# Reading one operand of VectorE's multiplications from PSUM, in a two-layer graph network on one core

## The chip, the cores and the metric

The kernel runs on one core of one Trainium2 chip. The metric is the device time of one execution in microseconds. TensorE multiplies matrices and writes PSUM, VectorE (DVE in the profile) and ScalarE (ACT) work element by element on SBUF and PSUM, GpSimd (POOL) issues the gathers, and SyncE (SP) issues the other transfers.

## What is computed

The reference is two layers of a relational graph convolution over 50,000 nodes with 128 features each, then a residual sum and a layer norm. There are 850,000 edges (50,000 of them self-loops), with 16 relations, whose matrices are combinations of 8 bases. Cut to what matters:

```python
def _rgcn_layer(h, src, dst, rel, basis, w_comp, loop_w, bias):
    W = jnp.einsum('rb,bio->rio', w_comp, basis)
    seg = dst.astype(jnp.int32) * N_REL + rel.astype(jnp.int32)
    agg = jax.ops.segment_sum(h[src], seg, num_segments=N_ENT * N_REL)
    agg = agg.reshape(N_ENT, N_REL, -1)
    msg = jnp.einsum('nri,rio->no', agg, W)
    out = msg + h @ loop_w + bias
    return jax.nn.relu(out)

h = _rgcn_layer(x, src, dst, edge_type, basis1, w_comp1, loop_w1, bias1)
h = _rgcn_layer(h, src, dst, edge_type, basis2, w_comp2, loop_w2, bias2)
out = _layernorm(x + h)
```

Edges are sorted by destination.

## The kernel before

Edges other than self-loops are cut into tiles of 128, and tiles into chunks of `K` = 10. A layer has 625 chunks, 6,250 tiles. For each tile POOL gathers the 128 source rows (line 250) into one of `GATHERS` = 4 buffers `g`, each a chunk long; the gathers of chunk c + 2 stand in the program at chunk c, and a gather waits until TensorE has read the same tile four chunks earlier.

A tile's destinations are at most `WN` = 12 neighbouring nodes. For each chunk, `hot_of` (lines 906 to 922) makes two things on VectorE. At line 909, `own`: for each edge, a 0/1 row that says which of the 12 nodes is its destination, by comparing `grid` (the numbers 0 to 11, a part of `col` in SBUF) with the edge's `key`. At line 916, `hot`: the product of `own` with the edge's 8 weights `pm`, one per basis, that is 960 numbers a partition. The program makes `hot` for chunk c two chunks early. TensorE multiplies a tile's gathered rows by its `hot` (line 1004) into a PSUM bank `pa`: 8 bases by 12 nodes, 96 columns; five tiles share a bank. VectorE then adds each tile's 96 columns into `ring` in SBUF at the place of its nodes (`add`, line 936).

`ring` holds three groups of 512 nodes. A group's share begins with its self-loops: `Group.own` (line 766) multiplies `wide` (the group's self-loop weights, spread over all partitions by a transfer of 1 MB from `CW`, four bases at a time) by `hT`, the transposed features of the group, broadcast over the four bases: 2,048 numbers a partition, twice a group, 98 groups a layer. When all chunks that touch a group are added, ScalarE copies its ring (line 783), TensorE multiplies by the bases (line 789) and by the loop matrix (line 794), ScalarE applies bias and relu (line 801), TensorE transposes back (line 813), and the rows are stored.

In the first layer, beside the chunks, VectorE also sorts edges and self-loops apart (`closed_up`, lines 317 to 330): it takes a bit of each word (line 326) into `bit` and copies by that predicate (line 329), 450 times each.

PSUM has eight banks of 512 columns. One is `pn`, for the bases. Seven turn as `pa`, handed out by `banks.take` (class `Turns`): it takes the oldest bank, and first emits the reading operations that were registered for that bank and have not been emitted yet, such as the adds of its five tiles. `Once` makes each of these run a single time, whether at its planned time or forced by `take`. Beside the tiles of a chunk, the weights of a batch of four chunks (`multiply`, two banks, copied out at line 678), the transposed features, the combined self-loop weights and the way back each take a bank.

The order of TensorE, POOL, VectorE and ScalarE is the order in which the program emits. Steps beside the chunks are put in a heap with the tile number at which they are due (`later`), and `go_on` emits those that are due after each tile; adds are emitted by `added_up_to`, some 25 tiles behind their matmul. Transfers on SP are ordered by a scheduler.

Of the kernel before, what the change touches and what calls it, by code (L numbers as in the profile page):

```python
# [40 lines left out]
F32 = mybir.dt.float32  # L41
I32 = mybir.dt.int32
BF16 = mybir.dt.bfloat16
# [5 lines left out]
PSUM = bass.MemoryType.PSUM  # L49
DRAM = bass.MemoryType.DRAM  # L50

P = 128
EPR = 850000
ROW = 10
WN = 12
K = P // WN
# [11 lines left out]
BANK = 512  # L68
WEIGHTS = AT * PER * 8
BITS_AT_ONCE = 224  # L70
# [6 lines left out]
BEHIND = 12  # L77
AFTER = 18
AT_ONCE = 4
# [10 lines left out]
def tile_rgcn_resnorm(  # L90
# [15 lines left out]
    nc = tc.nc  # L106
    N, D = x.shape
    NR, NB = w_comp1.shape
# [34 lines left out]
    consts = ctx.enter_context(tc.tile_pool(name="consts", bufs=1))  # L143
    col = consts.tile([P, P], F32, name="col")
# [3 lines left out]
    ident = consts.tile([P, P], F32, name="ident")  # L148
    nc.vector.tensor_scalar(ident, col, part, None, op0=OP.is_equal)

    grid = col[:, :WN]
    eps = consts.tile([P, 1], F32, name="eps")
    nc.vector.memset(eps, EPS)

# [64 lines left out]
                    left = less  # L219
            nc.vector.tensor_copy(split[:, n], mine)  # L220

    ps_a = ctx.enter_context(tc.tile_pool(name="ps_a", bufs=7, space=PSUM))
    ps_n = ctx.enter_context(tc.tile_pool(name="ps_n", bufs=1, space=PSUM))

    class Turns:
        def __init__(self, pool, name, count):
# [17 lines left out]
            if what is not None:  # L244
                what(*self.args)

    banks = Turns(ps_a, "pa", 7)

    def gather(to, of, idx):
        return nc.gpsimd.indirect_dma_start(  # L250
# [27 lines left out]
    picked = consts.tile([P, 5 * NG + 3 * len(ROWS)], F32, name="picked")  # L278
    ones = consts.tile([P, 1], F32, name="ones")
    place = consts.tile([P, RUN], F32, name="place")  # L280
    bit = consts.tile([P, BITS_AT_ONCE], I32, name="bit")

    odd_i = consts.tile([P, 1], I32, name="odd_i")
    nc.gpsimd.iota(odd_i, pattern=[[0, 1]], base=0, channel_multiplier=1)
# [318 lines left out]
    def chunked():  # L603
        with (
# [8 lines left out]
            def nodes(g):  # L613
                return min(GN, N - g * GN) // J
# [10 lines left out]
            class Weights:  # L625
                def __init__(self, c, n):
                    self.c, self.n = c, n
                    self.m = min(AT, 2 * (C - c)) * NR
                    self.keep = Once(self.kept)
# [58 lines left out]
            class Group:  # L688
                def __init__(self, g, of, n, copied):
                    self.g, self.of, self.n, self.copied = g, of, n, copied  # L690
                    self.m, self.cnt = nodes(g), nodes(g) * J
                    self.at = g % TURN * GN
                    self.wide, self.made = {}, False
                    self.keep, self.kept = Once(self.turned), Once(self.store, 0)
                    self.combined = Once(self.stored_comb)

# [55 lines left out]
                def widen(self, b):  # L752
# [7 lines left out]
                        ),  # L760
                    )

                def own(self, b):
                    cnt = self.cnt
                    assert self.g < TURN or self.copied[0] > self.g - TURN
                    nc.vector.tensor_tensor(  # L766
                        ring[:, b : b + AT_ONCE, self.at : self.at + cnt],
                        self.wide.pop(b)[:, :, :cnt],
                        self.hT[:, None, :cnt].to_broadcast([P, AT_ONCE, cnt]),
                        op=OP.mult,  # L770
                    )
                    self.made = b == NB - AT_ONCE
# [57 lines left out]
                        done(self.norm)  # L830
                        nc.sync.dma_start(of_group(out, g), self.t)

                def planned(self, later, free):
                    from_chunk = -(-(self.g * GN - NEAR) // (N // C)) - 1
                    start = K * from_chunk - 4
                    end = max(K * final(self.g) + K - 1 + BEHIND, free - AFTER + 1)
                    went = start - 2
                    if self.n == 0:
                        later(went - 78, self.load)
                        later(went - 66, self.turn)  # L840
                        later(went - 66 + BEHIND, self.keep)
                        later(went - 62, self.compare)
                        later(went - 48, self.combine)
                        later(went - 48 + BEHIND, self.combined)
                    else:
                        later(went - 40, self.load)
                    for i, b in enumerate(range(0, NB, AT_ONCE)):
                        later(went - 30 + 14 * i, self.widen, b)
                        later(went - 16 + 14 * i, self.own, b)
                    later(end, self.copy)  # L850
                    for b in range(NB):
                        later(end + AFTER + 2 * b, self.base, b)
                    end += AFTER + 2 * NB
                    later(end, self.loop)
                    later(end + BEHIND, self.relu)
                    later(end + BEHIND + AFTER, self.back)
                    later(end + 2 * BEHIND + AFTER, self.kept)
                    for step in range(1, 3 if self.n else 1):
                        later(end + 2 * BEHIND + AFTER + 3 * step, self.store, step)
                    return end + BEHIND  # L860
# [43 lines left out]
            for n, of in enumerate((x, H1)):  # L904

                def hot_of(c):
                    pm = batches[c // BATCH].pm
                    own = hp.tile([P, K, WN], BF16, name="own")
                    nc.vector.tensor_tensor(  # L909
                        own[:, : ks(c)],  # L910
                        grid[:, None, :].to_broadcast([P, ks(c), WN]),
                        key[:, c * K : c * K + ks(c), None].to_broadcast([P, ks(c), WN]),
                        op=OP.is_equal,
                    )
                    hot = hp.tile([P, K, NB, WN], F32, name="hot", bufs=4)
                    nc.vector.tensor_tensor(  # L916
                        hot[:, : ks(c)],
                        pm[:, c % BATCH * K : c % BATCH * K + ks(c), :, None].to_broadcast([P, ks(c), NB, WN]),
                        own[:, : ks(c), None, :].to_broadcast([P, ks(c), NB, WN]),
                        op=OP.mult,  # L920
                    )
                    hots[c] = hot
# [26 lines left out]
                def later(time, what, *args):  # L949
                    heapq.heappush(events, (time, len(order), what, args))  # L950
                    order.append(None)
# [17 lines left out]
                for batch in batches[1:]:  # L969
                    when = K * (batch.c - 3) + PER + 3  # L970
# [6 lines left out]
                free = 0  # L977
                for one in groups:
                    free = one.planned(later, free)
# [3 lines left out]
                for c in range(C):  # L983
# [16 lines left out]
                    for k in range(K):  # L1000
                        if k % PER == 0:
                            pa = banks.take(Once(added_up_to, c * K + k + PER - 1))
                        if k < ks(c):
                            nc.tensor.matmul(  # L1004
                                pa[:, k % PER * NB * WN : (k % PER + 1) * NB * WN],
                                g[:, k, :],
                                hot[:, k].rearrange("e b w -> e (b w)"),
                                start=True,
                                stop=True,
                            )  # L1010
                            behind.append((c * K + k + BEHIND, (c, k, pa)))
                        added_up_to(c * K + k - BEHIND)
                        if c or k >= BEHIND - 2:
                            go_on(c * K + k)
                    if n == 0 and c == 3:
                        beginning.close()
# [212 lines left out]
```

## Time and profile before

| | us |
|---|---|
| three timed executions | 18,116.25 to 18,146.69, median 18,145.05 |
| the profiled execution | 18,143.9 |
| its span, first to last instruction | 18,141.6 |

The profile is of one execution. A group's row names the line, engine, operation, tiles (out<-in) and count, then the busy time in us and the mean ns of one, then the time that the engine stood idle before them and what ended most of it. "issue" means that the profile shows nothing waited for, "remote" that the releaser is not known. A row of the timeline has the start, the length, what ran, how many in a row, and the idle time before the first. fp32 matmuls of lines 1004, 789, 794 and 664 show as two instructions each.

### The profile page before, as it was taken

What the parts mean: (1) busy time and instruction counts of PE and PEld (TensorE: products, weight loads), DVE (VectorE), ACT (ScalarE), POOL (GpSimd) and SP (SyncE); (2) the same over time, 40 slices, a digit from 0 to 9 for tenths busy, and PEclk for the clock granted to TensorE, in tenths of its full rate; (3) what the DMA queues carried; (4) which work ended last, traced back from release to release, by engine and by line L of the source; (5) the groups of instructions that cost most, each with busy time, mean ns of one, the idle gap of its engine ahead of it and who ended that gap; (6) DMA issues with size and microseconds to landing.
All of it is one profiled execution on the core that took longest, in us unless ns stands there. A gap on an engine that the chain in (4) does not pass through costs nothing.

```text
span 18141.6 us, 132343 instructions
## 1 busy us (share of the span) xinstructions
PE 8301.5 (46%) x31484; PEld 6157.8 (34%) x31484; DVE 6520.1 (36%) x18252; ACT 1406.4 (8%) x1864; POOL 12963.3 (71%) x12540
## 2 busy tenths in 40 slices
PE   3444444444444444444444444444444444445444
PEld 2333333333333333333333333333333333333333
DVE  4444444443333333333333333333333333333333
ACT  0000000000000000000000000000000000000000
POOL 6777777777777777777767777777777777777776
PEclk7666666666666666665655655655565556655565
DMA  3333333322222222222222222222222222222222
GB/s 100 95 93 92 93 94 94 94 90 88 80 85 84 85 84 85 85 85 81 84 79 80 81 81 79 81 84 76 81 84 78 81 81 81 81 81 81 81 81 67
DMA packets 793016, 1527.31 MB, mean 84 GB/s; under 512 B 229924, under 2 KB 296342, under 8 KB 792230
## 3 DMA queue, kind: packets, MB, share of 16 engines
q0 software_dynamic: 403552, 826.82, 15.8%
q1 hardware_dynamic: 386934, 691.33, 11.5%
q8 instruction: 260, 4.26, 0.1%
q14 instruction: 526, 4.31, 0.1%
q10 hardware_dynamic: 1744, 0.60, 0.0%
HBM read 1390.97 MB, written 126.86 MB: 84 GB/s over the span
## 4 chain that ended last, share of the span: by engine, by line
issue 37%; PE 22%; another core or an unknown queue 15%; POOL 14%; DMA 7%; DVE 3%; ACT 1%; DVEq 0%; POOLq 0%; ACTq 0%; SPq 0%
PE pa L1004 14%; POOL g L250 14%; PE pn L789 5%; DMA g<-H,src 4%; DMA g<-in_x_dram,src 3%; DVE ring L936 1%; PE pa L664 1%; ACT own L783 1%; PE pa L813 1%; PE pn L794 1%; DVE ring L766 1%; DVE word L329 0%; DVE bit L326 0%; DVEq L930 0%
## 5 line engine op out<-in xcount | busy, mean ns | idle before, releaser
L1004 PE MATMUL pa<-hot,g 128*128 128x96 f32 x25000 | 5869.2, 361 | 8329.8 <-issue 5856.8
L1004 PEld LDWEIGHTS pa<-hot,g 128*128 128x128 f32 x25000 | 5129.8, 269 | 10232.5 <-issue 7601.0
L250 POOL DMA_INDIRECT g<-in_x_dram,src x6250 | 6497.8, 1040 | 2549.3 <-issue 1150.2
L250 POOL DMA_INDIRECT g<-H,src x6250 | 6426.4, 1028 | 2549.6 <-issue 1167.7
L936 DVE TENSOR_TENSOR ring<-pa,ring 128x96 f32 x12500 | 3205.0, 256 | 10919.4 <-remote 5042.0
L789 PE MATMUL pn<-own,basis 128*128 128x512 f32 x3104 | 2062.1, 749 | 242.5 <-issue 193.9
L916 DVE TENSOR_TENSOR hot<-pm,own 128x960 f32<-128x960 f32 x1250 | 1457.5, 1166 | 90.8 <-remote 17.5
L783 ACT COPY own<-ring 128x4096 f32<-128x4096 f32 x194 | 699.4, 3605 | 5461.9 <-DVE ring L936 4142.0
L766 DVE TENSOR_TENSOR ring<-wide,hT 128x2048 f32<-128x2048 f32 x392 | 896.1, 2286 | 232.3 <-DMA wide<-CW 111.9
L789 PEld LDWEIGHTS pn<-own,basis 128*128 128x128 f32 x3104 | 601.6, 236 | 334.6 <-issue 287.0
L664 PE MATMUL pa<-each,is_rel 128*128 128x128 f32 x1570 | 375.3, 376 | 579.6 <-issue 380.6
L801 ACT ACTIVATE oT<-pn,bias_of 128x512 f32<-128x512 f32 x196 | 134.2, 685 | 6281.8 <-remote 2909.1
L664 PEld LDWEIGHTS pa<-each,is_rel 128*128 128x128 f32 x1570 | 312.7, 273 | 631.9 <-issue 467.7
L909 DVE TENSOR_TENSOR own<-col,key 128x120 bf16<-128x120 f32 x1250 | 341.9, 273 | 0.0
L813 PE MATMUL pa<-ident,oT 128*128 128x128 f32 (+1 forms) x784 | 215.5, 378 | 236.2 <-issue 190.1
L794 PE MATMUL pn<-hT,loop 128*128 128x512 f32 x392 | 251.8, 717 | 69.1 <-issue 69.1
L813 PEld LDWEIGHTS pa<-ident,oT 128*128 128x128 f32 (+1 forms) x784 | 147.8, 221 | 279.2 <-issue 271.5
L678 ACT COPY pm<-pa 128x192 f32<-128x192 f32 x628 | 142.7, 304 | 804.6 <-remote 635.0
L329 DVE COPY_PREDICATED word<-bit,word 128x224 int32<-128x224 int32 (+9 forms) x450 | 180.2, 400 | 37.6 <-DVE bit L326 11.5
L601 ACT ACTIVATE t<-t,nm,rs 128x128 f32<-128x128 f32 x392 | 161.3, 482 | 78.3 <-issue 36.1
L721 PE MATMUL pa<-ident,rows 128*128 128x128 f32 x392 | 102.2, 380 | 107.9 <-issue 71.2
L749 ACT COPY lrel<-pa 16x512 f32<-16x512 f32 x98 | 56.2, 574 | 1166.5 <-remote 599.9
(127 smaller groups left out, 1328.4 us busy)
## 6 DMA issues: line engine op xcount, KB each, us to landing
wide<-CW SPq DMA_DIRECT2D x388, 1024.0 KB
g<-in_x_dram,src POOLq DMA_INDIRECT x6250
g<-H,src POOLq DMA_INDIRECT x6250
rows<-in_x_dram SPq DMA_DIRECT2D x194, 256.0 KB
PM<-pm SPq DMA_DIRECT2D x157, 160.0 KB
pm<-PM SPq DMA_DIRECT2D x157, 160.0 KB
H1T<-oT SPq DMA_DIRECT2D x97, 256.0 KB
H<-t SPq DMA_DIRECT2D x97, 256.0 KB
```

The costliest lines, as they stand in the source:

```text
L250: return nc.gpsimd.indirect_dma_start(out=to, out_offset=None, in_=of, in_offset=bass.IndirectOffsetOnAxis(ap=idx, axis=0))
L329: moved = nc.vector.copy_predicated(word[:, a : a + k], bit[:, :k], word[:, a + step : a + step + k])
L664: nc.tensor.matmul(of[:, :, :, (j - j0) * NB : (j - j0 + 1) * NB], self.is_rel[:m, j * P : (j + 1) * P], each[:m], start=True, stop=True,)
L766: nc.vector.tensor_tensor(ring[:, b : b + AT_ONCE, self.at : self.at + cnt], self.wide.pop(b)[:, :, :cnt], self.hT[:, None, :cnt].to_broad ...
L783: nc.scalar.copy(self.sums, ring[:, :, at : at + cnt])
L789: nc.tensor.matmul(self.pn[:, : self.cnt], BASIS[:, b, :], self.sums[:, b, :], start=b == 0, stop=False)
L794: nc.tensor.matmul(self.pn[:, : self.cnt], LOOP, self.hT[:, : self.cnt], start=False, stop=True)
L813: nc.tensor.transpose(self.po[:m, j * D : (j + 1) * D], by_place[:, j, :], ident)
L909: nc.vector.tensor_tensor(own[:, : ks(c)], grid[:, None, :].to_broadcast([P, ks(c), WN]), key[:, c * K : c * K + ks(c), None].to_broadcast ...
L916: nc.vector.tensor_tensor(hot[:, : ks(c)], pm[:, c % BATCH * K : c % BATCH * K + ks(c), :, None].to_broadcast([P, ks(c), NB, WN]), own[:, ...
L936: nc.vector.tensor_tensor(into, pa[:, k % PER * NB * WN : (k % PER + 1) * NB * WN].rearrange("d (b w) -> d b w", w=WN), into, op=OP.add,)
L1004: nc.tensor.matmul(pa[:, k % PER * NB * WN : (k % PER + 1) * NB * WN], g[:, k, :], hot[:, k].rearrange("e b w -> e (b w)"), start=True, st ...
```

## The change

`grid` moves from SBUF into a PSUM bank of its own, `fixed`, which also holds `own` (two places that alternate by chunk, now 32-bit instead of bfloat16) and `bit`. So line 909 reads `grid` from that bank and writes `own` to it, line 916 reads `pm` from SBUF and `own` from PSUM, and line 329 reads its predicate from PSUM. For line 766 a new step `lay` on ScalarE copies the group's `hT` into a bank taken from the turning ones, once for each of the two multiplications of a group, 8 tiles ahead of it; the multiplication then reads `wide` from SBUF and the copy from PSUM, and is registered as that bank's reader. The turning banks become six. Steps of groups other than the first are due no earlier than tile 12, and in a layer's first chunk due steps are emitted after its last tile, where before none was.

```diff
-    grid = col[:, :WN]
...
-    ps_a = ctx.enter_context(tc.tile_pool(name="ps_a", bufs=7, space=PSUM))
+    ps_a = ctx.enter_context(tc.tile_pool(name="ps_a", bufs=6, space=PSUM))
+    ps_f = ctx.enter_context(tc.tile_pool(name="ps_f", bufs=1, space=PSUM))
+    fixed = ps_f.tile([P, BANK], F32, name="fixed")
     ps_n = ctx.enter_context(tc.tile_pool(name="ps_n", bufs=1, space=PSUM))
+
+    grid = fixed[:, :WN]
+    nc.vector.tensor_copy(grid, col[:, :WN])
...
-    banks = Turns(ps_a, "pa", 7)
+    banks = Turns(ps_a, "pa", 6)
...
-    bit = consts.tile([P, BITS_AT_ONCE], I32, name="bit")
+    bit = fixed[:, WN + 2 * K * WN : WN + 2 * K * WN + BITS_AT_ONCE].bitcast(I32)
...
-                    self.wide, self.made = {}, False
+                    self.wide, self.laid, self.made = {}, {}, False
+                    self.owns = {b: Once(self.own, b) for b in range(0, NB, AT_ONCE)}
...
+                def lay(self, b):
+                    self.laid[b] = banks.take(self.owns[b])
+                    nc.scalar.copy(self.laid[b][:, : self.cnt], self.hT[:, : self.cnt])
+
                 def own(self, b):
...
-                        self.hT[:, None, :cnt].to_broadcast([P, AT_ONCE, cnt]),
+                        self.laid.pop(b)[:, None, :cnt].to_broadcast([P, AT_ONCE, cnt]),
...
-                def planned(self, later, free):
+                def planned(self, queue, free):
+                    def later(when, *what):
+                        queue(max(when, BEHIND) if self.g else when, *what)
+
...
-                        later(went - 16 + 14 * i, self.own, b)
+                        later(went - 24 + 14 * i, self.lay, b)
+                        later(went - 16 + 14 * i, self.owns[b])
...
-                    own = hp.tile([P, K, WN], BF16, name="own")
+                    at = WN + c % 2 * K * WN
+                    own = fixed[:, at : at + K * WN].rearrange("e (k w) -> e k w", w=WN)
...
-                        if c or k >= BEHIND - 2:
+                        if c or k == K - 1:
                             go_on(c * K + k)
```

## The prediction

> **What bounds the kernel now.** I read the page's busy times first, then its groups, then the gathers' own rows, then waits and a timeline. The sum is made against the profiled execution: 18,143.9 us, of which the span is 18,141.6; the median of the three timed runs, 18,145.05, is the same within 0.01%.
>
> ```profile
> PE 8301.5 (46%) x31484; PEld 6157.8 (34%) x31484; DVE 6520.1 (36%) x18252; ACT 1406.4 (8%) x1864; POOL 12963.3 (71%) x12540
> ...
> L250 POOL DMA_INDIRECT g<-in_x_dram,src x6250 | 6497.8, 1040 | 2549.3 <-issue 1150.2
> L250 POOL DMA_INDIRECT g<-H,src x6250 | 6426.4, 1028 | 2549.6 <-issue 1167.7
> L936 DVE TENSOR_TENSOR ring<-pa,ring 128x96 f32 x12500 | 3205.0, 256 | 10919.4 <-remote 5042.0
> ...
> L916 DVE TENSOR_TENSOR hot<-pm,own 128x960 f32<-128x960 f32 x1250 | 1457.5, 1166 | 90.8 <-remote 17.5
> ...
> L766 DVE TENSOR_TENSOR ring<-wide,hT 128x2048 f32<-128x2048 f32 x392 | 896.1, 2286 | 232.3 <-DMA wide<-CW 111.9
> ...
> L909 DVE TENSOR_TENSOR own<-col,key 128x120 bf16<-128x120 f32 x1250 | 341.9, 273 | 0.0
> ```
>
> POOL is the busiest engine, and nearly all it does is 12,500 gathers. Their own rows, and a timeline stretch in the second layer:
>
> ```profile
> L250 POOL DMA_INDIRECT g<-in_x_dram,src x6250: 939/947/3060, 46.0 to 9117.1; - x196
> L250 POOL DMA_INDIRECT g<-H,src x6250: 939/947/3058, 9152.5 to 18093.2; - x196
> ```
> ```profile
> 12007.69 1.13 DVE L936 TENSOR_TENSOR ring<-pa,ring 128x96 f32 x4 [11.10 <-PE pa L1004]
> 12008.34 0.94 POOL L250 DMA_INDIRECT g<-H,src  x1 [0.30 <-DMA g<-H,src]
> ...
> 12008.74 0.27 DVE L909 TENSOR_TENSOR own<-col,key 128x120 bf16<-128x120 f32 x1
> 12009.04 1.16 DVE L916 TENSOR_TENSOR hot<-pm,own 128x960 f32<-128x960 f32 x1
> 12009.59 1.43 POOL L250 DMA_INDIRECT g<-H,src  x1 [0.30 <-issue]
> ...
> 12011.33 0.95 POOL L250 DMA_INDIRECT g<-H,src  x1 [0.30 <-issue]
> ```
>
> A gather takes 947 ns at the median (939 at least, 3,060 at most), and one follows another after 0.30 us: 1.25 us start to start. So 12,500 x 1.25 = 15,625 us would be enough. The rest is two things. The gathers' busy time is 6497.8 + 6426.4 = 12,924, which is 12,924 - 12,500 x 0.947 = 1,087 us more than the median gather would need. Their idle time is 5,099, which is 5,099 - 12,500 x 0.303 = 1,311 us more than the pipeline's own gap. 15,625 + 1,087 + 1,311 = 18,023; the first gather starts at 46 and the last one starts 48 us before the end, which leaves some 25 us for POOL's few other instructions.
>
> Where the 1,087 comes from is seen in the stretch: the gather at 12009.59 began while L916 ran, and ended 0.48 us late. The gather at 12008.34 began while L936 ran, and took 0.94. L916 reads two tiles in SBUF, L936 reads one of its two in PSUM. The long multiplication does the same, harder:
>
> ```profile
> 10413.85 0.94 POOL L250 DMA_INDIRECT g<-H,src  x1 [0.30 <-issue]
> ...
> 10418.55 2.29 DVE L766 TENSOR_TENSOR ring<-wide,hT 128x2048 f32<-128x2048 f32 x1
> 10418.85 2.81 POOL L250 DMA_INDIRECT g<-H,src  x1 [0.30 <-remote]
> 10420.87 0.37 SPq L754 DMA_DIRECT2D wide<-CW  x1
> 10420.88 0.84 DVE L936 TENSOR_TENSOR ring<-pa,ring 128x96 f32 x3
> ```
>
> L766 ends at 10420.84; the gather that met it ends at 10421.66, 0.82 us after it, late by 2.81 - 0.947 = 1.86.
>
> The 1,311 us of waits are of another kind: TensorE falls behind and POOL runs out of free buffers (four of ten tiles, so at most 40 tiles ahead).
>
> ```profile
> 10403.00:10455.00 52.00, 32.57 (x139) 24.04 (x139) 27.88 (x80) 6.24 (x7) 39.87 (x37) 0.73 0.32 99
> 10455.00:10495.00 40.00, 4.78 (x15) 4.02 (x14) 3.84 (x12) 0.69 (x1) 26.59 (x28) 0.50 0.23 65
> ```
> ```profile
> 10487.40 0.32 PE L1004 MATMUL pa<-hot,g 128*128 128x96 f32 x1 [2.48 <-issue]
> ...
> 10495.35 0.94 POOL L250 DMA_INDIRECT g<-H,src  x1 [5.39 <-remote]
> ```
>
> The columns of the windows are PE, PEld, DVE, ACT, POOL, each busy us (instructions), then the granted clock. In the 40 us from 10455 the clock was 0.50, TensorE did 15 matmuls (a tile needs two) and POOL 28 gathers, until a gather waited 5.39 us. Such stretches decide how much of a faster POOL is kept.
>
> **What the change does, part by part.**
>
> *L916, L909, L766 read one operand from PSUM.* Nothing is removed from VectorE. What goes, if the operand's place is what counts, is the lateness they give the gathers. Its size by geometry: a gather starts every 1.25 us, so an operation of d us catches one with probability d/1.25 and holds it d/2 on average, as long as d < 1.25; a longer one always catches one and holds it d - 0.62. L916: 1.166 x 1.166 / 2.5 = 0.54 us, x 1,250 = 680. L766: 2.286 - 0.62 = 1.66, x 392 = 652. L909: 0.273 x 0.273 / 2.5 = 0.03, x 1,250 = 37. That is 1,369, a quarter over the 1,087 that are there, so these three explain all of it; other two-input operations are short or few. I take 1,040 (96%).
>
> *Their own duration.* Two rows of 96 elements tell it, that of L936 above and this one:
>
> ```profile
> L777 DVE TENSOR_TENSOR ring<-ring 128x96 f32<-128x96 f32 x64 | 16.7, 260 | 2.2
> ```
>
> L936 takes 256 ns with one operand in PSUM, L777 260 with both in SBUF: no change. L909 now also writes the bank that it reads, which no row shows; even twice its 273 ns would be 342 us on an engine that idles 64% of the span, cover enough unless TensorE waits for the `hot` it makes. [...]
>
> *`lay`: 392 copies SBUF to PSUM on ScalarE.* The nearest row has the same 512 columns, out of PSUM:
>
> ```profile
> L821 ACT COPY t<-pa 128x512 f32<-128x512 f32 x97 | 57.0, 587 | 810.5 <-remote 601.3 <-PE pa L1004 199.2 <-PE pa L721 7.9
> ```
>
> 392 x 0.587 = 230 us on an engine that is 8% busy. It stands 8 tiles (10 us) ahead of the multiplication; behind it on ScalarE wait L801, L678 and the like, 0.6 us later. Free on the path.
>
> *Six banks instead of seven, and 392 more takes.* `take` forces the adds of the oldest bank out earlier, so TensorE runs with less room ahead of VectorE. The nearest row for a bank that is not free in time:
>
> ```profile
> DVE ring L936 <- remote: 5042.0, 367, 48.9
> ...
> DVE ring L936 <- PE pa L1004: 3639.2, 816, 30.2
> ...
> PE pa L1004 <- ACT pm L678: 523.6, 42, 51.1
> ```
>
> The columns are us in total, times, the longest. 314 banks that L678 empties (two for each of 157 batches) cost 523.6, 1.67 us a take; 392 more takes at that price are 654 us of TensorE, half of which POOL would feel. The other bound is 0, since VectorE empties the new banks within its own order, as it does those of L936. I take 30 us on POOL's path.
>
> *The start.* `bit` in PSUM takes the second SBUF input from 450 short L329s; events before tile 12 move by a few tiles once a layer. Within 20 us either way; 0 taken. POOL's order of gathers is untouched, and so is each queue's list of transfers.
>
> *How much of 1,040 is kept.* Where TensorE is the later one, an earlier POOL only waits longer at the 40-tile limit. All and nothing are the bounds. As a measure I take the time that L936 stood waiting for TensorE by the two rows above, 5042.0 (releaser not shown) + 3639.2 = 8,681 us, 48% of the span: 52% kept, 541 us. The stretches of slow TensorE seem to come in time, so 3% less time has 3% less of the 1,311: 39 us. Sum: 18,144 - 541 - 39 + 30 = 17,594, say 17,590.
>
> **Rivals.**
>
> *All kept, 17,100.* TensorE catches up between slow stretches every time (32.57 us busy out of 52 in the first window, at 139 matmuls for 37 gathers). 18,144 - 1,040 = 17,104, and down to 17,030 with fewer slow stretches. Against it: the lateness falls mostly while TensorE catches up, as after 10403.
>
> *TensorE paces everything, about 18,100.* POOL reaches the limit sooner and waits; 0 to 15% kept. Against it: POOL idles only 1,311 over its own gaps.
>
> *The operand's place is not what counts, 18,144.* A long VectorE operation may hold the gather whatever it reads; the trace has few long ones with a PSUM operand. Against it: the gather at 10413.85 and that at 12008.34 started inside runs of L936 and lost nothing. [...]
>
> *Banks run short, 18,350: slower.* Place: TensorE's wait for a bank at L1004, just while it catches up. If each of the 392 takes costs w us and half lands on POOL, the gain of 541 is gone at w = 2.8; at w = 4 it is 784 lost, 18,387, at 3.8 18,350. For it: L678's banks cost 1.67 now with seven. Against it: VectorE is idle 64%, and banks of L936 are not among the long waits of TensorE.
>
> **How the numbers follow.** The forecast has 0.52, all kept 0.20, TensorE paces 0.12, the operand does not count 0.05, banks 0.11. The likeliest one's own range is 17,350 to 17,850. Both ends of "how much is kept" belong to the range: 17,050 to 18,080 leaves out the slower rival and the farthest of no change. Faster by more than 0.2% (36 us, about what a measurement of this kernel can tell): 0.52 + 0.20 + 0.10 of the pacing case = 0.82. Within 0.2%: 0.02 + 0.05 = 0.07. Slower: 0.11.
>
> **What would show it.** Gathers' mean near 950 ns instead of 1,034, with a maximum far below 3 us; that alone tells whether the operand's place counts. POOL's idle time near 5,600 us (5,099 + 499 not kept): if it stays at 5,100, all was kept; at 6,100, TensorE paces. The rows of L916 and L766 within 3% of 1,166 and 2,286 ns. TensorE's waits for ScalarE or VectorE at L1004 under 700 us, or the banks bite. I am wrong in the main step if gathers still take over 1,000 ns on average.

## The result and the profile after

| | kernel before, us | changed kernel, us |
|---|---|---|
| median of the timed runs | 18,145.11 (18,116.25 to 18,146.69, 6 runs) | 18,063.03 (18,059.16 to 18,074.16, 6 runs) |
| span of the profiled execution | 18,141.6 | 18,063.9 |

The ratio is 0.9958, with a 95% interval of 0.9945 to 0.9971: the change gained 82 us, where 555 were forecast. The page of the changed kernel has the busy times and the groups that answer to those of before (line 254 is the old 250, 950 the old 936, 930 the old 916, 775 the old 766, 923 the old 909, 1018 the old 1004; 770 is the new copy of features, `lay`):

```profile
PE 8315.7 (46%) x31484; PEld 6301.1 (35%) x31484; DVE 6563.7 (36%) x18253; ACT 1621.0 (9%) x2256; POOL 11861.6 (66%) x12540
```
```profile
L254 POOL DMA_INDIRECT g<-in_x_dram,src x6250 | 5929.4, 949 | 3046.5 <-issue 1432.7 <-remote 810.4 <-PE pa L1018 639.6
L254 POOL DMA_INDIRECT g<-H,src x6250 | 5895.2, 943 | 3045.9 <-issue 1428.8 <-remote 793.1 <-PE pa L1018 655.5
L1018 PE MATMUL pa<-hot,g 128*128 128x96 f32 x25000 | 5704.8, 361 | 7613.1 <-issue 5607.3 <-ACT pm L682 536.1 <-DVE ring L775 307.2
...
L930 DVE TENSOR_TENSOR hot<-pm,fixed 128x960 f32<-128x960 f32 x1250 | 1443.0, 1154 | 78.9 <-remote 19.2 <-issue 6.0 <-DVE fixed L923 2.6
...
L775 DVE TENSOR_TENSOR ring<-wide,pa 128x2048 f32<-128x2048 f32 x392 | 893.7, 2280 | 84.1 <-issue 28.8 <-ACT pa L770 14.2 <-DMA wide<-CW 12.0
...
L923 DVE TENSOR_TENSOR fixed<-fixed,key 128x120 f32<-128x120 f32 x1250 | 350.4, 280 | 0.1
...
L770 ACT COPY pa<-hT 128x512 f32<-128x512 f32 x392 | 230.8, 589 | 3035.4 <-DVE ring L950 1349.5 <-issue 954.9 <-PE pa L1018 432.0
```
The gathers' own rows give least, median and greatest duration:
```profile
L254 POOL DMA_INDIRECT g<-in_x_dram,src x6250: 938/944/1612, 47.9 to 9070.3; - x196
L254 POOL DMA_INDIRECT g<-H,src x6250: 938/944/1022, 9110.5 to 18011.4; - x196
```

The gathers did what the change was made to do. Their busy time fell from 12,924 to 5929.4 + 5895.2 = 11,825 us, by 1,100; the greatest duration in the second layer fell from 3,058 ns to 1,022. But POOL's idle time before them rose from 5,099 to 3046.5 + 3045.9 = 6,092, by 994. Nine tenths of what the gathers gave came back as waiting, spread over the whole run. The waits of the changed kernel, us in total, times and the longest:

```profile
DVE ring L950 <- PE pa L1018: 5215.2, 1059, 22.6
DVE ring L950 <- remote: 4149.8, 567, 28.9
POOL g L254 <- issue: 2861.5, 9120, 3.6
...
POOL g L254 <- remote: 1603.5, 1256, 8.9
...
POOL g L254 <- PE pa L1018: 1295.0, 1639, 8.3
```

POOL waits more for TensorE (1,295 us against 717 before) and more for something whose releaser is not shown (1,603 against 1,076). This looks like the rival "TensorE paces everything, about 18,100", to the number: 6,100 us of idle time was named for it. A stretch of the changed kernel's timeline shows what TensorE does in such times (start, length, engine, what, how many, idle time before):

```profile
9001.58 0.28 PEld L1018 LDWEIGHTS pa<-hot,g 128*128 128x128 f32 x1 [1.23 <-DMA g<-in_x_dram,src]
9002.27 0.32 PE L1018 MATMUL pa<-hot,g 128*128 128x96 f32 x1 [1.03 <-DMA g<-in_x_dram,src]
9002.97 0.29 PEld L1018 LDWEIGHTS pa<-hot,g 128*128 128x128 f32 x1 [1.10 <-issue]
9003.00 0.50 PE L1018 MATMUL pa<-hot,g 128*128 128x96 f32 x1 [0.41 <-issue]
9003.22 0.94 POOL L254 DMA_INDIRECT g<-in_x_dram,src  x1 [1.79 <-remote]
9003.67 0.29 PEld L1018 LDWEIGHTS pa<-hot,g 128*128 128x128 f32 x1 [0.41 <-issue]
```

TensorE's instructions come 0.70 us apart (9001.58, 9002.27, 9002.97, 9003.67), the last two with nothing shown that they wait for; steps of 0.70 us and its multiples, within 20 ns, add up to some 7 ms of the run, before and after the change. Theory 1 was therefore: TensorE, with these stretches, sets the pace by the work that it has to do. The experiments contradict it.

### The profile page after: what moved, and what is told of

Same layout as the page of the kernel before. It is cut to its first block, busy times and chain, and to the rows that moved or that the text cites. A ratio compares the mean times of both kernels' runs of the same rounds, so it can differ in the third digit from the quotient of the medians.

```text
span 18063.9 us, 132710 instructions
## 1 busy us (share of the span) xinstructions
PE 8315.7 (46%) x31484; PEld 6301.1 (35%) x31484; DVE 6563.7 (36%) x18253; ACT 1621.0 (9%) x2256; POOL 11861.6 (66%) x12540
## 4 chain that ended last, share of the span: by engine, by line
issue 37%; PE 28%; another core or an unknown queue 16%; POOL 8%; DVE 5%; DMA 3%; ACT 1%; DVEq 1%; POOLq 0%; ACTq 0%; SPq 0%
PE pa L1018 18%; POOL g L254 8%; PE pn L798 8%; DVE ring L950 2%; DMA g<-H,src 2%; DVE ring L775 1%; PE pa L668 1%; PE pn L803 1%; DMA g<-in_x_dram,src 1%; ACT own L792 0%; PE pa L822 0%; DVE fixed L330 0%; DVEq L944 0%; DVE word L333 0%
## 5 line engine op out<-in xcount | busy, mean ns | idle before, releaser
L1018 PE MATMUL pa<-hot,g 128*128 128x96 f32 x25000 | 5704.8, 361 | 7613.1 <-issue 5607.3
L1018 PEld LDWEIGHTS pa<-hot,g 128*128 128x128 f32 x25000 | 5201.3, 276 | 9323.7 <-issue 7321.4
L254 POOL DMA_INDIRECT g<-in_x_dram,src x6250 | 5929.4, 949 | 3046.5 <-issue 1432.7
L254 POOL DMA_INDIRECT g<-H,src x6250 | 5895.2, 943 | 3045.9 <-issue 1428.8
L950 DVE TENSOR_TENSOR ring<-pa,ring 128x96 f32 x12500 | 3212.4, 257 | 10941.4 <-PE pa L1018 5215.2
L798 PE MATMUL pn<-own,basis 128*128 128x512 f32 x3104 | 2237.5, 799 | 508.1 <-issue 486.0
L930 DVE TENSOR_TENSOR hot<-pm,fixed 128x960 f32<-128x960 f32 x1250 | 1443.0, 1154 | 78.9 <-remote 19.2
L775 DVE TENSOR_TENSOR ring<-wide,pa 128x2048 f32<-128x2048 f32 x392 | 893.7, 2280 | 84.1 <-issue 28.8
L770 ACT COPY pa<-hT 128x512 f32<-128x512 f32 x392 | 230.8, 589 | 3035.4 <-DVE ring L950 1349.5
L726 PEld LDWEIGHTS pa<-ident,rows 128*128 128x128 f32 x392 | 74.6, 223 | 845.1 <-ACT t L830 457.0
L923 DVE TENSOR_TENSOR fixed<-fixed,key 128x120 f32<-128x120 f32 x1250 | 350.4, 280 | 0.1
```

Of the source, the lines that this page charges most:

```text
L254: return nc.gpsimd.indirect_dma_start(out=to, out_offset=None, in_=of, in_offset=bass.IndirectOffsetOnAxis(ap=idx, axis=0))
L770: nc.scalar.copy(self.laid[b][:, : self.cnt], self.hT[:, : self.cnt])
L775: nc.vector.tensor_tensor(ring[:, b : b + AT_ONCE, self.at : self.at + cnt], self.wide.pop(b)[:, :, :cnt], self.laid.pop(b)[:, None, :cnt] ...
L798: nc.tensor.matmul(self.pn[:, : self.cnt], BASIS[:, b, :], self.sums[:, b, :], start=b == 0, stop=False)
L923: nc.vector.tensor_tensor(own[:, : ks(c)], grid[:, None, :].to_broadcast([P, ks(c), WN]), key[:, c * K : c * K + ks(c), None].to_broadcast ...
L930: nc.vector.tensor_tensor(hot[:, : ks(c)], pm[:, c % BATCH * K : c % BATCH * K + ks(c), :, None].to_broadcast([P, ks(c), NB, WN]), own[:, ...
```

## The experiments

Runs that were sent together ran on one chip, with the kernel before beside them. In which set they ran turned out to matter more than the kernels:

| runs sent together | kernel before, us |
|---|---|
| the result | 18,145 |
| first: a_onebase, b_onebase, b_sixbanks, a_fixedonly | 18,260 |
| second: a_onepass, b_onepass, a_warm2, a_warm4 | 16,912 |
| third: a_plain, b_plain, a_onepass_r, a_fixedonly_r | 16,917 |
| fourth: a_onepass_c, a_warm4_c, a_copiesonly | 18,147 |
| fifth: a_halfgathers, a_halfproducts | 18,145 |
| sixth: a_signals | 16,917 |

Chips with 18,150 or 18,260 us are called paced chips here, those with 16,900 free chips. That the chip itself makes the difference is not shown: the record gives the number 7 to the chip of the fourth runs (18,147) and to that of the sixth (16,917), and whether that is one chip at two times is not known. Ratios are to the kernel before on the same chip, with their 95% interval.

### TensorE's products with the basis taken away (first)

```diff
...
-                    for b in range(NB):
+                    for b in range(1):
                         later(end + AFTER + 2 * b, self.base, b)
```


> The changed kernel with seven of the eight products with the basis left out per group (2,744 of TensorE's 512-column products at 799 ns, 2,190 us of its busy time; they take no turning bank). Theory 1 (TensorE sets the pace of the changed kernel, POOL waits for it): the time falls to POOL's own pace, 11,825 us of gathers and an idle time of 5,100 us or a little more, 16,950 to 17,300 us, and the gathers stay at 943 to 950 ns. Rival 2 (the lost bank and the 392 new takes hold the chain up, VectorE or ScalarE being late with a bank): these waits stay, 17,700 us or more. Rival 3 (POOL has a pace of its own near 18,060 us whatever its gathers take): 18,000 us or more.

> The kernel before with the same seven of eight products left out. Theory 1: POOL keeps its slow gathers (12,900 us busy) and loses only its waits for TensorE, 17,600 to 18,000 us, so that the changed kernel under the same cut is 600 to 1,000 us faster than this one. Rival 2 and rival 3: the two kernels under the cut stay within 200 us of each other.

Measured: a_onebase 18,157.55 us, 0.9945 (0.9928 to 0.9962), b_onebase 18,189.73, 0.9962 (0.9948 to 0.9976). Seven of eight products with the basis, 1.9 ms of TensorE's busy time, are left out and the time stays. The changed kernel's rows:

```profile
L254 POOL DMA_INDIRECT g<-in_x_dram,src x6250 | 5933.6, 949 | 3089.3 <-issue 1436.7 <-remote 980.5 <-PE pa L1018 549.5
L254 POOL DMA_INDIRECT g<-H,src x6250 | 5906.7, 945 | 3071.5 <-issue 1437.0 <-remote 904.9 <-PE pa L1018 635.8
L1018 PE MATMUL pa<-hot,g 128*128 128x96 f32 x25000 | 5838.5, 373 | 9202.7 <-issue 7107.7 <-ACT pm L682 447.2 <-ACT lrel L754 352.6
```

POOL's idle time is 6,161 us, as with all products. TensorE's "issue" is 7,107.7 us, 1,500 more than in the profile of the result: what it no longer does, it waits. TensorE's amount of work is not the limit, and theory 1 as first put falls.

### One bank less, and the fixed bank alone (first)

```diff
-    ps_a = ctx.enter_context(tc.tile_pool(name="ps_a", bufs=7, space=PSUM))
+    ps_a = ctx.enter_context(tc.tile_pool(name="ps_a", bufs=6, space=PSUM))
...
-    banks = Turns(ps_a, "pa", 7)
+    banks = Turns(ps_a, "pa", 6)
```


> The kernel before with six turning banks in place of seven, nothing else changed. Theory 1: additions are forced earlier, but the chain has slack there: 18,145 to 18,250 us. Rival 2: the lost bank alone costs a good part of the 990 us that POOL's idle time grew by: 18,450 us or more.

Measured: 1.0003 (0.9994 to 1.0013). A lost bank alone costs nothing that can be measured on this paced chip; on a free chip it was not run alone.

```diff
-                        self.laid.pop(b)[:, None, :cnt].to_broadcast([P, AT_ONCE, cnt]),
+                        self.hT[:, None, :cnt].to_broadcast([P, AT_ONCE, cnt]),
...
-                        later(went - 24 + 14 * i, self.lay, b)
```


> The changed kernel with the node numbers and comparisons in the fixed bank, but the self-loop multiplication reading its features from SBUF again, without the copies to a bank (six turning banks). Its gathers get back the excess beside the self-loop multiplication, some 860 of 1,087 us, so 12,650 to 12,750 us busy. Theory 1: POOL's idle time gives way by nearly as much, since TensorE sets the pace: 18,050 to 18,160 us. Rival 2 (the copies' takes are what costs): 17,300 to 17,700 us less the slower gathers, that is below 18,000 us. Rival 3: 18,050 to 18,150 us as well.

Measured: 18,216.49 us, 0.9977 (0.9967 to 0.9986). The gathers were 12,346 us busy, fewer than the 12,650 to 12,750 expected, and POOL 5,740 idle: 500 us slower gathers than with the whole change cost next to nothing. That is what theory 1 said, but by the runs above the amount of TensorE's work is not the reason.

### Other ways to relieve or to load TensorE (second)

```diff
-                                g[:, k, :],
-                                hot[:, k].rearrange("e b w -> e (b w)"),
+                                g[:, k, :].bitcast(BF16)[:, 1 : 2 * D : 2],
+                                hot[:, k].rearrange("e b w -> e (b w)").bitcast(BF16)[:, 1 : 2 * NB * WN : 2],
```


> The changed kernel with each tile's product made from the upper 16 bits of features and weights, as bf16 (precision is left out): one pair of weight load and product per tile where there were two, 25,000 pairs become 12,500; every other instruction stays. Theory 1, restated after the first four runs (TensorE paces the changed kernel, but by its tile products and their stretches of one instruction per 0.70 us, not by its busy time): the time falls to POOL's own pace, a ratio to the kernel before of 0.935 to 0.955, with gathers at 943 to 950 ns and POOL's idle time under 5,300 us. Rival 3 (POOL or its transfers have a pace of their own near the present time): a ratio of 0.99 or more.

> The kernel before with the same one-pass products. Theory 1 restated: its gathers stay slow (12,900 us busy), it loses its waits for TensorE only, a ratio of 0.975 to 0.995, so that the changed kernel is 600 to 1,100 us faster under the same cut. Rival 3: 0.99 or more for both, within 100 us of each other.

```diff
...
                             pa = banks.take(Once(added_up_to, c * K + k + PER - 1))
+                            for _ in range(2):
+                                nc.tensor.matmul(pa[:, :512], idb, warmth[:, :512], start=True, stop=True)
```


> The changed kernel with two useless bf16 products of 512 columns (their result is overwritten) at the start of each turning bank of tiles, 5,000 in all. If the slow stretches come because TensorE is used too thinly (theory 1a): fewer of them, higher granted clock, a ratio of 0.95 to 0.985. If TensorE's total of work paces (theory 1b): 0.995 to 1.03. Rival 3: unchanged, 0.99 to 1.00.

> The same with four useless products per bank, 10,000 in all. Theory 1a: a ratio of 0.94 to 0.98, below that with two. Theory 1b: 1.02 to 1.15. Rival 3: 0.99 to 1.01.

Measured: a_onepass 15,820.90 us, 0.9355 (0.9339 to 0.9370); b_onepass 16,952.84, 1.0024 (1.0014 to 1.0033); a_warm2 15,806.82, 0.9347 (0.9331 to 0.9362); a_warm4 15,805.59, 0.9345 (0.9330 to 0.9361). All three versions of the changed kernel take the same time, whether TensorE has less or more to do, and the one of the kernel before gains nothing. The kernel before itself took 1,233 us less in these runs than beside the result. So these runs alone say nothing on one pass or on dense work; the changed kernel itself had to be run on such a chip.

### The two kernels again, on a free chip (third)

> The changed kernel once more. In the last four runs the kernel before took 16,912 us, where it had taken 18,145 and 18,260 us, and its one-pass version showed hardly any of TensorE's 0.70 us steps. Theory 4: the chips differ in these stretches of TensorE, and the change is worth what TensorE leaves of it. Where the kernel before takes about 16,900 us, the changed kernel takes 15,790 to 15,830 us (0.934 to 0.937) with POOL's idle time under 4,000 us; where it takes 18,100 us or more, 0.993 to 0.998. Theory 1 as first put (TensorE's tile products pace it everywhere, and one pass or useless products relieve it): 0.985 to 1.00 on either chip.

> The kernel before once more, for its profile on the same chip as the run above: a ratio of 0.998 to 1.002. Theory 4: gathers 1,020 to 1,045 ns either way; where it takes 16,900 us, TensorE's idle time with no releaser is under 1,000 us and it waits for the gathers' transfers; where it takes 18,100 us, that idle time is above 5,000 us.

Measured: the changed kernel 15,801.53 us, 0.9340 (0.9324 to 0.9356); the kernel before again, 1.0001 (0.9992 to 1.0011). The gathers of the kernel before on this chip, then of the changed kernel:

```profile
L250 POOL DMA_INDIRECT g<-in_x_dram,src x6250 | 6513.6, 1042 | 1937.6 <-issue 1126.4 <-PE pa L1004 368.1 <-DMA g<-in_x_dram,src 364.6
L250 POOL DMA_INDIRECT g<-H,src x6250 | 6456.5, 1033 | 1934.5 <-issue 1273.1 <-PE pa L1004 364.8 <-DMA g<-H,src 274.0
```
```profile
L1018 PE MATMUL pa<-hot,g 128*128 128x96 f32 x25000 | 7440.4, 415 | 5799.9 <-DMA g<-H,src 2796.7 <-DMA g<-in_x_dram,src 2526.4 <-DVE ring L950 354.1
L254 POOL DMA_INDIRECT g<-in_x_dram,src x6250 | 5932.5, 949 | 1942.3 <-issue 1123.3 <-PE pa L1018 391.3 <-DMA g<-in_x_dram,src 341.4
L254 POOL DMA_INDIRECT g<-H,src x6250 | 5897.2, 944 | 1932.0 <-issue 1213.3 <-PE pa L1018 387.4 <-DMA g<-H,src 290.2
```

Here the gathers' idle time is 3,872 us before and 3,874 after, that is 0.31 us for each of 12,500: POOL hardly stands still but for its own gap. Busy time fell from 6513.6 + 6456.5 = 12,970 to 5932.5 + 5897.2 = 11,830, by 1,140, and the span from 16,941.3 to 15,803.5, by 1,138. What the gathers gave is what the kernel gained, all of it.

The changed kernel on this chip, at the same time of the run, shows TensorE close behind POOL. Two weight loads come for each gather (x2), and they wait for the transfer of a gather a few tiles back:

```profile
9000.83 0.95 POOL L254 DMA_INDIRECT g<-H,src  x1 [0.30 <-issue]
9000.91 0.30 PEld L1018 LDWEIGHTS pa<-hot,g 128*128 128x128 f32 x2 [0.69 <-DMA g<-H,src]
...
9002.09 0.94 POOL L254 DMA_INDIRECT g<-H,src  x1 [0.30 <-issue]
9002.11 0.30 PEld L1018 LDWEIGHTS pa<-hot,g 128*128 128x128 f32 x2 [0.91 <-DMA g<-H,src]
```

Counted over the trace (gathers begun less tile products ended), POOL is 3 tiles ahead of TensorE at the median here, and 26 on the chip of the result.

> The version without the copies of features again. Theory 4 on a chip without TensorE's slow stretches: the gathers' excess beside the self-loop multiplication, some 860 us, comes back in full, 16,600 to 16,720 us (0.981 to 0.989), of which the 1,250 comparisons and weights' products gain only 200 to 260 us; on a chip with them 0.996 to 0.999, as before.

> The changed kernel with one-pass tile products again. Theory 4 on a chip with TensorE's slow stretches: half of the tile instructions are gone, so the stretches shrink by a third or more, 0.94 to 0.975; on a chip without them 0.934 to 0.937, as the changed kernel itself. If the stretches are not per instruction: 0.99 or more where the kernel before takes 18,100 us.

Measured: a_fixedonly_r 16,357.67 us, 0.9667 (0.9651 to 0.9683). The direction was right and the share wrong: by the rows below, the copies give 6209.9 + 6173.0 - 11,830 = 553 of the 1,140 us, and the fixed bank the other 587. a_onepass_r took 15,820.23 us, 0.9351 (0.9335 to 0.9366): on a free chip one pass gains nothing.

```profile
L254 POOL DMA_INDIRECT g<-in_x_dram,src x6250 | 6209.9, 994 | 1941.0 <-issue 1151.0 <-PE pa L1017 386.4 <-DMA g<-in_x_dram,src 318.9
L254 POOL DMA_INDIRECT g<-H,src x6250 | 6173.0, 988 | 1934.8 <-issue 1293.3 <-PE pa L1017 357.5 <-DMA g<-H,src 269.4
```

### The same relief on a paced chip (fourth)

> One-pass tile products in the changed kernel, for a chip with TensorE's slow stretches. There, if a stretch costs 0.70 us for every instruction that TensorE starts (12,500 pairs fewer): 0.94 to 0.975. If it costs time whatever TensorE has to do, as when seven of eight products with the basis were left out: 0.99 to 1.00. On a chip where the kernel before takes 16,900 us: 0.934 to 0.937.

> Four useless bf16 products of 512 columns per bank in the changed kernel, for a chip with the stretches. There, if dense work keeps TensorE from falling into them (the granted clock rises): 0.94 to 0.985; if each instruction costs the same: 1.01 to 1.10; if time is lost whatever it has to do: 0.99 to 1.01. On a chip where the kernel before takes 16,900 us: 0.934 to 0.937.

> The changed kernel with the copies of features to a bank alone: node numbers, comparisons and bits stay in SBUF, and seven banks turn as before. On a chip where the kernel before takes 16,900 us: half of the change's gain, since the other half (560 us) came with the fixed bank: a ratio of 0.964 to 0.970, 16,330 to 16,420 us. On a chip with the stretches: 0.996 to 1.000.

Measured: a_onepass_c 17,927.76 us, 0.9881 (0.9865 to 0.9898); a_warm4_c 18,146.08, 1.0000 (0.9990 to 1.0009); a_copiesonly 18,050.39, 0.9945 (0.9929 to 0.9962). Against the changed kernel's 0.9958 on its own paced chip, half of the tile instructions gone is worth some 0.8%, and 10,000 more products cost some 0.4%. The copies alone, with seven banks, stand within 0.2% of the whole change, on another paced chip: there one half of the change is worth as much as both.

### Half of the gathers, half of the products (fifth)

```diff
-                        for k in range(ks(to)):
+                        for k in range(0, ks(to), 2):
                             gather(rows[buffer][:, k, :], of, src[:, to * K + k : to * K + k + 1])
...
-                                g[:, k, :],
+                                g[:, k - k % 2, :],
```


> The changed kernel with every second gather left out (6,250 of 12,500; a tile product without a gather of its own reads its neighbour's rows), all other work kept. On a chip where the kernel before takes 18,100 us: if TensorE's work or its stretches set the pace at 1.44 us a tile, 17,000 us or more; if it is something that goes with each gather (its transfers and their signals), under 14,000 us. On a chip where it takes 16,900 us: TensorE or VectorE paces, 10,000 to 13,000 us.

```diff
-                        if k < ks(c):
+                        if k < ks(c) and k % 2 == 0:
                             nc.tensor.matmul(
```


> The changed kernel with all gathers, but the product and the addition of every second tile left out (6,250 of 12,500 each). On a chip where the kernel before takes 18,100 us: if TensorE's stretches set the pace tile by tile, POOL's own pace comes through, 15,800 to 16,500 us; if it is something that goes with each gather, 17,500 us or more. On a chip where it takes 16,900 us: 15,780 to 15,820 us, POOL's pace.

Measured, beside a kernel before of 18,144.50 us: a_halfgathers 9,653.31 us, 0.5320 (0.5305 to 0.5336); a_halfproducts 17,850.14, 0.9838 (0.9809 to 0.9866). The rows with half of the gathers, then with half of the products:

```profile
L1018 PE MATMUL pa<-hot,g 128*128 128x96 f32 x25000 | 4593.8, 338 | 2133.5 <-issue 1347.9 <-DVE ring L775 262.2 <-ACT pm L682 111.6
...
L254 POOL DMA_INDIRECT g<-in_x_dram,src x3125 | 2972.7, 951 | 1789.9 <-issue 707.5 <-PE pa L1018 667.7 <-remote 296.3
L254 POOL DMA_INDIRECT g<-H,src x3125 | 2947.9, 943 | 1647.8 <-issue 756.7 <-remote 437.7 <-PE pa L1018 393.8
```
```profile
L254 POOL DMA_INDIRECT g<-in_x_dram,src x6250 | 5948.6, 952 | 2923.9 <-issue 1712.1 <-remote 844.6 <-PE pa L1018 254.4
L254 POOL DMA_INDIRECT g<-H,src x6250 | 5911.2, 946 | 2929.7 <-issue 1686.1 <-remote 793.3 <-PE pa L1018 330.4
```

So the amount of TensorE's or VectorE's work alone is not the limit. TensorE did all 25,000 tile instructions, and VectorE all its work, in 9,653 us on a paced chip; half of TensorE's and VectorE's tiles left out changed the time by no more than 1.2%. The time goes with the gathers: 18,064 / 12,500 = 1.45 us each with the whole change, 17,850 / 12,500 = 1.43 with half of the products, 9,642 / 6,250 = 1.54 with half of the gathers, though POOL's own part of a gather is 0.95 + 0.30 in all of them. These are means: in the profile of the result one gather follows another after 1.25 us at the median, and 1,396 of the 12,500 stand over 0.6 us.

What those gathers wait for can be read from the traces, and it is TensorE after all. A gather waits for a semaphore of TensorE (a counter: in the trace of the changed kernel 14,985 of TensorE's instructions raise this one), and for the transfers' semaphore that it shares with the gather eight before it (there are eight of these, each named by 1,562 or 1,563 gathers). With half of the products, 6,263 gathers name the transfers' semaphore alone: they stood 20 us in all beyond the gap of 0.305 us. The 6,230 that name TensorE's stood 2,011 us. In the profile of the result, 1,308 of the 1,396 long waits end with a gather that starts 245 to 275 ns after an update of TensorE's semaphore; a window of the same width 0.3 us earlier holds such an update 5 times. And these updates come late by the trace's times. On the free chip of the third runs practically all of them come within 20 ns of the end of an instruction that makes them, for both kernels; on the chip of the result 9% do, where 97% of VectorE's and over 99% of ScalarE's still do. Where a gather stood long, the product 40 tiles earlier, which frees its buffer, had ended 22 us before at the median. So POOL's freed time went into waiting for signals of TensorE, and less work on TensorE hardly brings them sooner.

### More signals without gathers (sixth)

What goes with each gather, beside POOL's instruction, are its transfers and the signals that they give: 226,454 updates from transfers in the changed kernel's trace of the third runs. This run adds signals:

```diff
+                    for i in range(2):
+                        nc.scalar.dma_start(more[(2 * c + i) % 4], x[:P, :16])
```


> The changed kernel with 2,500 more small transfers, two a chunk, issued by ScalarE into tiles that nobody reads (8 KB each; over sixteen queues each should signal sixteen times, 40,000 signals beside the 226,454 that the undisturbed trace holds). On a chip where the kernel before takes 18,100 us: if the pace is that of the transfers' signals (18,064 / 226,454 = 80 ns each), 20,500 to 21,500 us; if it goes with the gathers in another way, 18,050 to 18,300 us. On a chip where it takes 16,900 us: 15,790 to 15,900 us.

Measured: 15,807.15 us, 0.9345 (0.9318 to 0.9372). It fell on a free chip, where 38,717 more updates from transfers cost nothing that can be measured (the changed kernel was 0.9340); on a paced chip this was not tried, so the run does not tell what paces there.

## Why the prediction was right or wrong

*The operand's place counts: right.* Gathers' mean 949 and 943 ns where "near 950" was named, busy time 1,100 us less where 1,040 was taken, and on a free chip 1,140. So "the operand's place is not what counts" is refuted. The copies show it alone, since only the place changes there; in the fixed bank `own` also went from bfloat16 to 32-bit, and no run separates the two. The geometry that sized it held roughly: it gave L916 with L909 717 us and L766 652; the two halves measured 587 and 553, which are 18% and 15% less.

*Own durations unchanged: right.* 1,154 and 2,280 ns against 1,166 and 2,286. One operation that was not priced writes the bank now: `bit` of 224 numbers, 309 ns before, 390 after, 290 times:

```profile
L330 DVE TENSOR_SCALAR fixed<-word 128x224 int32<-128x224 int32 x290 | 113.0, 390 | 13.4 <-DVE word L333 4.6 <-remote 1.7 <-issue 1.6
```
That is 23 us on an engine that is idle 64% of the span.

*`lay`: right.* 230.8 us at 589 ns, where 587 was taken, and on a free chip POOL's idle time is the same with and without it (3,874 and 1941.0 + 1934.8 = 3,876 us).

*Six banks and 392 takes: right to price it low, by a sign that could not tell.* One bank less alone was 1.0003. The sign named for a shortage, over 700 us of TensorE's waits for ScalarE or VectorE at L1004, was badly chosen: these waits add up to 973 us before the change and to 1,530 after it, and 435 on a free chip. TensorE's wait at L1018 for L775, the new turn of a bank, is 307.2 us in the profile after, inside the bound of 654; on a free chip TensorE's product row names 354.1 us for L950's banks, and none of it reached POOL, whose idle time differed by 2 us. "Banks run short", which made the kernel slower, is refuted.

*How much of 1,040 is kept: wrong, and this is the step that failed.* It said that 52% is kept, because L936 stood waiting for TensorE 48% of the span. On the chip of the result 82 us were kept, 8% of 1,040, and on a free chip all. The 52% took VectorE's share of waiting for the chance that TensorE is the later one. What the runs showed in its place: on that chip POOL waits for TensorE's semaphore, whose updates come late, and the mean from gather to gather stays near 1.44 us, where POOL alone needs 1.25. POOL's waits beyond its own gap grew from 1,291 to 2,284 us, so 993 of the 1,100 us saved became waiting; on a free chip POOL's idle time is 0.31 us a gather and all is kept. The kernel before, with gathers of 1.034 + 0.30 us on average, was already held by it, though its own 12,500 gathers would need 16,900 us only, which is what it takes on a free chip.

*Slow stretches come in time, so 39 us less: wrong in sign.* POOL's idle time grew by 994 us. *The start* moved by 2 us (the first gather at 47.9 instead of 46.0), inside the 20 allowed.

*The rivals.* "TensorE paces everything, about 18,100" has the number and half of the cause: POOL does wait for TensorE, but not because TensorE has too much to do. The runs with fewer products with the basis, one pass, and half of the products all took TensorE's work away on paced chips and moved the time by 1.2% at most, as ratios beside the changed kernel's 0.9958. "All kept, 17,100" holds on free chips, where the gathers' saving came entire; its reason, that TensorE catches up between slow stretches, was not put to the test there, since the 0.70 us steps add up to 0.3 ms only.

*What misled both the forecast and theory 1* was what the rows of waits do not say. The prediction counted 5,042.0 us of "remote" as waiting for TensorE, and that was right: updates of TensorE's semaphore ended 5,028 of them, with no instruction ending close enough to be named. So they did all of POOL's 1,603 us of "remote" in the changed kernel. But such a wait does not say that TensorE has too much work. "issue" tells less still. Counted in each trace, the updates of semaphores, those of them that come from transfers, and the share of TensorE's updates that come within 20 ns of the end of an instruction that makes them:

```
kernel and runs                  span us     updates   from transfers   TensorE's in time
before, the result              18,141.6      61,692           38,876                 24%
changed, the result             18,063.9      56,008           34,010                  9%
a_onepass_c (fourth)            17,926.9      44,284           25,458                 11%
b_plain (third)                 16,941.3     259,732          226,446                100%
a_plain (third)                 15,803.5     259,964          226,454                100%
a_signals (sixth)               15,807.7     298,594          265,171                100%
```

The same changed kernel leaves 259,964 updates on a free chip and 56,008 on a paced one, though both traces hold all 132,710 instructions. Nearly four fifths of the updates, mostly those of transfers, are missing there, so a wait that such an update ended is put down to "issue". In the free chip's trace, TensorE's two largest waits at L1018 are for the gathers' transfers (2,796.7 + 2,526.4); in the paced one the largest is "issue" with 5,607.3, and what ended it cannot be read.

*What stays open* is why TensorE's updates come late on paced chips, and why the time there falls with the gathers and hardly with TensorE's work. The gathers' data are not late by the traces of the result: where 16 packets of 4 KB stand between the end of one gather and that of the next, the last of them ends 1.18 us after POOL's instruction at the median before the change and 1.25 us after it, while POOL is 26 tiles ahead of TensorE in the changed kernel there and 3 on a free chip. Nor are the transfers' signals, as far as the trace kept them: they come 1.33 us after it at the median on the chip of the result (29,125 of some 200,000) and 1.43 on a free one. Whether TensorE itself is held up there or its updates alone is not shown. Nor is it shown whether the recording, which has so many updates fewer there, takes part in it: every run carries a span and a clock, and none was made without a recording.

## What to carry to other kernels

Where POOL issues gathers back to back, look at what VectorE runs beside the long ones: two inputs in SBUF held a gather up (to 3,058 ns in the second layer, 1,022 with one input in PSUM), and with one of them moved the two long operations took 1,154 and 2,280 ns, where they had taken 1,166 and 2,286. Before a share of a gain is taken off because an engine "waits", ask whether the update that ended the wait is in the trace, and whether it came when its producer ended; "issue" in a trace that lost most of its updates is a gap in the evidence. And take work away from the suspected engine before believing that its work paces: a time that stays, as it did within 1.2% with half of the products left out, says that the waits have another reason than the amount of work.

## What the runs showed of the hardware that was not expected

The same kernel takes 16,912 to 16,917 us in some sets of runs and 18,145 to 18,260 in others, with 0.04 to 0.22% between the lowest and the highest run of a set, and this change is worth 6.6% in the one kind and 0.4% in the other. With all gathers the changed kernel takes 1.43 to 1.45 us for each of them on average on paced chips, however much TensorE has to do. TensorE's instructions 0.70 us apart are a mark of the same runs: some 7 ms by the count above, and 0.3 ms in the same kernel on a free chip. So are TensorE's late updates: 9% within 20 ns of an instruction's end in the changed kernel, against 100%.

Useless dense work raised TensorE's granted clock without any gain in time: 0.602 for the changed kernel on the chip of the result, 0.687 with 10,000 more products on a paced chip, at 18,063 and 18,146 us; 0.617 and 0.727 on free chips, at 15,802 and 15,806. Nearly 39,000 more updates from transfers cost next to nothing on a free chip: 15,807 us against 15,802.
